# Moving a seventh of a depthwise convolution's taps from VectorE to ScalarE and adding DMAs, in a fused attention and ConvNeXt kernel

## The chip, the cores and the metric

The kernel runs on one core of one Trainium2 chip. The metric is the device time of one execution in microseconds (us), lower is better. The time before is 3349.05 us, the median of three runs (3346.46 to 3350.15). The engines are named as in the profile: PE is the matrix engine, PEld its weight loads, DVE is VectorE, ACT is ScalarE, POOL is GpSimd and SP is SyncE. POOL and SP do hardly anything here but issue DMAs.

## The reference, cut to what matters

Two layers run one after the other on a batch of 8 images of 384 channels and 32 x 32 pixels, all in float32.

```python
# layer 0: attention and MLP over the 1024 pixels ("tokens") of an image
xn = layernorm(xf, g1, beta1)                  # over the 384 channels
q, k, v = split(xn @ w_qkv.T + b_qkv)          # 8 heads of 48
out = softmax(q @ k.T * SCALE) @ v
x1 = out @ w_proj.T + b_proj + xf
h = gelu(layernorm(x1, g2, beta2) @ w_fc1.T + b_fc1)    # 384 -> 1536
x = x1 + h @ w_fc2.T + b_fc2                            # 1536 -> 384
# layer 1: ConvNeXt block
y = depthwise_conv_7x7(x, dw_w) + dw_b         # 49 taps, each channel by itself
y = layernorm(y, ln_w, ln_b)
y = gelu(y @ w1 + b1)                          # 384 -> 1536
gx = sqrt(sum over pixels of y ** 2); nx = gx / (mean of gx + eps)
y = grn_gamma * (y * nx) + grn_beta + y
out = x + y @ w2 + b2                          # 1536 -> 384
```

## The kernel before, in words

**Layout.** Channels lie on the 128 partitions, in CT = 3 channel tiles (`ct`), and the 1024 pixels of an image along the free axis, in two halves of NH = 512. A float32 matmul over 512 columns is two MATMUL rows in the profile. The images are worked off one after the other, and the two layers overlap: while PE does layer 0 of image b, the convolution of image b-1 runs beside it. For an image in the middle PE's order is: `values` and `qk` (the projections), `attention` (64 steps of scores and products, four pairs of heads for each half of the queries), `mlp` (fc1 of half 0, then of half 1, then fc2), `grn_up` and `grn_down` of the image before (layer 1's two matmuls). fc2, w1 and w2 are done by fast-matrix-product forms (`by_thirds`, `grn_up`), which need extra sums on DVE and adding DMAs on POOL.

**The plan.** The program is written in a fixed order for each engine; every engine then runs its own list in order and waits on semaphores. Work beside the matmuls is written as Python generators, and the class `Flow` decides where their instructions are put: `flow.pe(us)` moves a planned clock on by the planned time of a matmul (U = 0.857 us for 512 columns) and steps every chain that has come due. `yield 3.4` means that the chain's next instructions are put 3.4 planned us further on between the matmuls. A chain that was spawned as paced keeps its rhythm by that clock. `flow.finish(chain)` puts all that is left of a chain at once. The numbers behind `yield` are therefore guesses of a latency: when one is too short, the engine that gets the next instruction stands and waits with all that is queued behind it.

**The convolution.** `pad` holds the image with a border of 3. `convolution` makes 49 taps for each of the 3 channel tiles. A tap is one DVE instruction over all 1024 pixels, `acc = window * tap + acc`, 147 in all for an image, put `us` planned us apart and taken from the tiles in turn. It starts after `grn_up` (`start_conv`) and has to be done by the end of fc1 of the next image, where `next_norms` finishes it. The last image has none to overlap with: `last_convolution` works in two parts, rows 0 to 12 and rows 13 to 31, beside fc2 and the layer 1 of image 6 (`last`, which lies in the tile that held the qkv weights).

**The layernorms.** `layernorm` sums the three channel tiles on DVE, sums over the partitions with a matmul by a matrix of ones (`token_sums`), subtracts the mean (DVE), squares (ACT), sums again, takes Ln and Exp on ACT, and multiplies on DVE. With `fold` a DMA on POOL's queue first adds one half of the partitions to the other, and the matmuls have 64 rows and 64 columns, so that those of two pixel halves lie in different parts of the array. `abreast` runs both pixel halves side by side and stretches the waits by `factor`. Three layernorms occur for an image: ln1 (before `values`), ln2 (before fc1) and ln3 (after the convolution). ln3 stood unfolded and at the beginning of fc2.

**The averages.** `average` divides one pair of heads by its softmax sums: ACT and DVE add two PSUM banks, then come the sums by DMA to 128 partitions, a reciprocal on DVE, two more DMA steps through DRAM, and a multiplication on DVE. Its three waits were 2.8, 2.0 and 2.4. `ORDER[-1]` is the pair that comes last in a half; `proj` follows close behind it.

**Tags.** A tile pool hands out its buffers in turn by tag, and an instruction that writes a buffer waits until its last reader is done. `three.tile(..., tag="res")` had 3 buffers of 128 x 512.

Of the kernel before, what the change touches and what calls it, by code (L numbers as in the profile page):

```python
# [51 lines left out]
P = 128  # L52
# [14 lines left out]
U = 0.857  # L67
SCALE = HD ** -0.5
# [82 lines left out]
def block_kernel(  # L151
# [25 lines left out]
    flow = Flow()  # L177
    s_fc2 = dram.tile([P, len(FORMS), 4 * P], F32, tag="s_fc2", bufs=1, name="s_fc2")
# [188 lines left out]
    def token_sums(t, name, fold):  # L367

        width = t.shape[-1]
        if fold is None:
            total = o_tile(name)[:, :width]
            nc.tensor.matmul(out=total, lhsT=ones, rhs=t, start=True, stop=True)  # L374
            flow.pe(U * width / NH)
            return [(total, slice(0, width))]
        rows = [slice(0, 64), slice(64, P)]
        parts = [(fold, slice(0, width))]
        if fold == "columns":
            parts = [(j, slice(j * width // 2, (j + 1) * width // 2)) for j in range(2)]  # L380
        for j, cols in parts:
            nc.gpsimd.dma_start(out=t[rows[j], cols], in_=t[rows[1 - j], cols], accum_op=ALU.add)
        yield 3.4
        totals = []
        for j, cols in parts:
            total = o_tile(f"{name}_{j}")[:, : cols.stop - cols.start]
            for i in rows:
                nc.tensor.matmul(out=total[i, :], lhsT=ones[rows[j], :64], rhs=t[rows[j], cols], start=True, stop=True)
            flow.pe(U * width / NH / 2)
            totals.append((total, cols))  # L390
        return totals

    def layernorm(src, dst, h, eps, g, name, switch, spare=None, spaced=False, slow=1.0, fold=None, gentle=False):
# [17 lines left out]
        totals = yield from token_sums(a, f"{name}_sum{h}", fold)  # L411
# [20 lines left out]
        totals = yield from token_sums(squares[0], f"{name}_var{h}", fold)  # L432
# [23 lines left out]
    def abreast(*args, places=averages, fold=True, gentle=False, factor=1.4):  # L456

        chains = [
            layernorm(*args[:2], h, *args[2:], spare=places if h else None, fold=h if fold else None, gentle=gentle)
            for h in range(2)  # L460
        ]
        while chains:
            waits = []
            for chain in list(chains):
                wait = next(chain, None)
                if wait is None:
                    chains.remove(chain)
                else:
                    waits.append(wait)
            if waits:  # L470
                yield factor * max(waits)
# [75 lines left out]
    def average(b, qh, m, outs, sums, backs):  # L547


        tag = f"{b}_{qh}_{m}"  # L550
        nc.scalar.copy(attn[:, m, :], outs[0])  # L551
        yield 0.6
        nc.vector.tensor_tensor(attn[:, m, :], outs[1], attn[:, m, :], ALU.add)  # L553
        at = (qh * NP + m) * 8
        part = sums[:, at : at + 8]
        rows = attn[HD : HD + 65 : 64, m, :]
        nc.sync.dma_start(out=part, in_=rows.rearrange("j (a e) -> j a e", e=8))
        yield 2.8
        inv = small.tile([P, 8], F32, tag="inv", name=f"inv_{tag}")
        nc.vector.reciprocal(inv, part)  # L560
        back = backs[m] = dram.tile([2, NH], F32, tag=f"back{m}", name=f"back_{tag}")
        nc.sync.dma_start(out=back.rearrange("j (a e) -> (j a) e", e=8), in_=inv)
        if m == NP - 1:
            return
        while NP - 1 not in backs:
            yield 1.0
        for i, (own, other) in enumerate(pieces(lambda k: attn[:, k, :])):
            if i // 2 == m:
                nc.sync.dma_start(out=other, in_=own)
        yield 2.0  # L570
        r = two.tile([P, NH], F32, tag="r", name=f"r_{tag}")
        for j in range(2):
            nc.sync.dma_start(out=r[64 * j : 64 * j + HD, :], in_=back[j : j + 1, :].to_broadcast((HD, NH)))
            head = (2 * m + j) // CT
            nc.sync.dma_start(
                out=r[64 * j + HD : 64 * j + 64, :], in_=backs[NP - 1][head : head + 1, :].to_broadcast((16, NH))
            )
        yield 2.4
        nc.vector.tensor_tensor(attn[:, m, :], attn[:, m, :], r, ALU.mult)  # L579

    def attention(b, xt, qT, kT, last_tile, first):
# [44 lines left out]
        for n in range(len(steps) + 2):  # L626
# [4 lines left out]
            if n >= 2:  # L631
                product(*steps[n - 2], ps.pop(n - 2))
            if n - 2 == len(steps) // 2 + 6:
# [6 lines left out]
                slow = 1.4 if b in (1, B - 1) else 1.0  # L640
                ln = layernorm(xt, xn, 0, eps0, "g2", f"ln2_{b}", False, spaced=True, slow=slow, fold="columns")
                ln = flow.spawn(ln)

        def rest():
# [6 lines left out]
            proj(b, xt, 1)  # L651

# [65 lines left out]
    def mlp(b, xt, xn, weights, tag, ln, rest, before_fc2):  # L718
# [5 lines left out]
        for m in range(HT):  # L724
            gelu_half(hid, m, 0, xn, weights, wa, f"fc1_{b}")
            if m == 3 and rest:
                rest()
                slow = 1.2 if b == 1 else 1.0
                ln = flow.spawn(layernorm(xt, xn, 1, eps0, "g2", f"ln2_{b}", True, slow=slow))
        flow.finish(ln)  # L730
# [118 lines left out]
    def mlp_by_halves(b, xt, xn, weights, ln, rest, between):  # L849

        hid = one.tile([P, HT * N], F32, tag="big", name=f"hid_{b}").rearrange("p (m n) -> p m n", m=HT)
        for h in range(2):
            wa, wb = f"fc1_{b}_{h}", f"fc2_{b}_{h}"
            flow.finish(ln)
            for m in range(HT):
# [6 lines left out]
                if m == 6 and h == 0:  # L862
# [17 lines left out]
    def convolution(acc, us, slow=0, y0=0, y1=H, ready=tuple(range(CT))):  # L880
# [5 lines left out]
        while min(done) < KS * KS:  # L886
            left = [c for c in ready if done[c] < KS * KS]
# [12 lines left out]
            yield 2.43 if n <= CT * slow else us  # L900

# [78 lines left out]
    def grn_down_straight(b, y, kept, weights, tag, index, todo):  # L980
# [5 lines left out]
        def load():  # L986
            if len(res) < len(todo):
                r, part = todo[len(res)]
                t = three.tile([P, NH], F32, tag="res", name=f"res_{b}_{r}_{part.start}")[:, : part.stop - part.start]
# [165 lines left out]
    def prepare(weights, aside):  # L1155
# [25 lines left out]
        def spare(name):  # L1181
            return three.tile([P, NH], F32, tag="res", name=name)
# [122 lines left out]
    def main():  # L1305
# [41 lines left out]
        state = {"xn": xn, "conv": None, "acc": None, "norm1": None, "norm3": None}  # L1347
        kept = {}

        def start_conv(b, us, slow=0):  # L1350
            state["acc"] = one.tile([P, CT, N], F32, tag="acc", name=f"acc_{b}")
            state["conv"] = flow.spawn(convolution(state["acc"], us, slow), paced=True)

        def next_norms(b, ln=None):

            if b > 0:
                acc = state["acc"]
                flow.finish(state["conv"])
                norm = abreast(acc, acc, eps1, "lnw", f"ln3_{b - 1}", True, fold=False)
                norm = sequence(norm, block_differences(acc)) if b < B - 1 else after(ln, norm)  # L1360
                state["norm3"] = flow.spawn(norm)
# [22 lines left out]
        def last_convolution(h, ct, ln=None):  # L1384
            if ct < 0:
                next_norms(B - 1, ln)
                return
            ready[h].append(ct)
            if ct == 0:
                rows = (LAST[0].stop // W, H) if h else (0, LAST[0].stop // W)  # L1390
                conv = convolution(last, 0.86 if h else 0.6, 0, *rows, ready[h])
# [4 lines left out]
        for b in range(B):  # L1396
# [6 lines left out]
            if b < B - 1:  # L1403
                mlp(b, xt, xn, weights, b, ln2, rest, lambda: next_norms(b))
# [6 lines left out]
            if b == 0:  # L1411
                xt = load_x(b + 1, "x")
                flow.finish(preparing)
                start_conv(b, 1.6)
# [5 lines left out]
            if b < B - 1:  # L1420
                y, gx = grn_up(b - 1, acc, weights, b - 1)
                start_conv(b, 1.5 if b == B - 2 else 1.8, 10)
                scale = flow.spawn(grn_scale(b - 1, gx, weights, b - 1, y))
                next_values(b + 1)
                flow.finish(scale)
                grn_down(b - 1, y, xt, weights, b - 1, b - 1)
                xt = load_x(b + 1, "x")
# [35 lines left out]
    def exact_path():  # L1463

        load_wqkv(nc.scalar, nc.scalar)
        with tc.For_i(0, B) as b:
# [11 lines left out]
            mlp("x", xt, xn, weights, "x", ln, None, None)  # L1478
# [111 lines left out]
```

## Time and profile before

| what | from the profile before |
|---|---|
| profiled execution, its own time | 3348.34 us (span 3346.6 us) |
| PE busy | 3303.6 us, 99% of the span |
| DVE busy | 2550.6 us, 76% |
| ACT busy | 1421.0 us, 42% |
| POOL busy | 208.1 us, 6% |
| taps of images 0 to 6 (L897, 128 x 1024) | 1008 rows, 1230.6 us busy, 1276 ns each |
| taps of image 7 (L897, 128 x 416 and 128 x 608) | 288 rows, 193.7 us busy |
| from the start of qk to the next one, image 1 | 350.13 to 760.90: 410.8 us |
| the same, image 2 | 760.90 to 1165.17: 404.3 us |
| the same, image 3 | 1165.17 to 1569.43: 404.3 us |
| from the start of image 7's qk to the end | 2782.04 to 3346.6: 564.6 us |

The span is counted from the first to the last instruction. A busy PE row is modelled at its end, so the distance from one start to the next tells what a matmul costs: about 0.43 us for a row of 512 columns. Idle time of an engine that is not last anywhere costs nothing.

### The profile page before, as it was taken

The page shows a single profiled execution, that of the slowest core. Times are in us where ns is not written, and L with a number is a line of the kernel's source. Part 1 is how long each engine was busy: PE and PEld are TensorE (multiplying, and loading weights), DVE is VectorE, ACT ScalarE, POOL GpSimd, SP SyncE. Part 2 cuts the span into 40 slices and gives each one's busy share as a digit, 9 for nine tenths or more (in the row PEclk, how much of TensorE's full clock was granted, in tenths as well). Part 3 has the DMA queues.
Part 4 walks back from the last instruction along what each step waited for, and adds up shares of the span by engine and source line. Part 5 has one row for each costly group of instructions (what it writes and reads, how often), then busy time and mean ns, then how long its engine had stood idle before and what let it go on. Part 6 is the DMA issues. An engine that isn't in the chain of part 4 may idle for free.

```text
span 3346.6 us, 37477 instructions
## 1 busy us (share of the span) xinstructions
PE 3303.6 (99%) x14282; PEld 1416.7 (42%) x14282; DVE 2550.6 (76%) x3133; ACT 1421.0 (42%) x1884; POOL 208.1 (6%) x243
## 2 busy tenths in 40 slices
PE   8999999999999999999999999999999999999999
PEld 4344434443344433444334443444434444334455
DVE  4344788887877878779797796967888779989950
ACT  3442453444534354352552625426254353522641
POOL 2121000100000000100001000010000110000000
PEclk9999999999999999999999999999999999999999
DMA  5336102642125410445005350062501633023231
GB/s 185 111 105 148 52 20 57 158 102 63 25 70 146 115 47 20 105 122 135 20 16 131 96 140 17 17 157 80 128 18 37 170 83 95 20 56 90 62 98 50
DMA packets 151243, 281.59 MB, mean 84 GB/s; under 512 B 35216, under 2 KB 41232, under 8 KB 150672
## 3 DMA queue, kind: packets, MB, share of 16 engines
q1 hardware_dynamic: 114704, 201.32, 19.6%
q0 software_dynamic: 36064, 77.08, 11.9%
q8 instruction: 115, 1.88, 0.2%
q10 hardware_dynamic: 288, 0.71, 0.1%
q14 instruction: 72, 0.59, 0.1%
HBM read 181.52 MB, written 33.82 MB: 64 GB/s over the span
## 4 chain that ended last, share of the span: by engine, by line
PE 87%; DVE 10%; DMA 2%; issue 1%; ACT 0%; SPq 0%; POOL 0%; DVEq 0%; POOLq 0%
PE o L612 12%; PE s L592 12%; PE fc L345 12%; PE h L352 10%; PE fc_p L352 10%; PE o_p L352 9%; PE qk L332 6%; DVE wqkv L897 4%; PE v L521 4%; PE o L1000 4%; PE proj L535 3%; DVE acc L897 3%; PE h_last L1044 1%; PE qk_last L345 1%; PE ln_var L374 1%
## 5 line engine op out<-in xcount | busy, mean ns | idle before, releaser
L897 DVE SCALAR_TENSOR_TENSOR acc<-pad,vec,acc 128x1024 f32<-128x1024 f32 x1008 | 1230.6, 1276 | 0.0
L601 ACT ACTIVATE p<-s 128x1024 f32<-128x1024 f32 x512 | 523.6, 1024 | 380.6 <-PE s L592 378.4
L592 PE MATMUL s<-qk 48*64 48x512 f32 x4096 | 544.0, 592 | 1.6 <-ACT qk L495 1.5
L612 PE MATMUL o<-p,v 64*64 64x512 f32 x4096 | 538.9, 590 | 0.0
L345 PE MATMUL fc<-xn,fc 128*128 128x512 f32 x1152 | 500.4, 593 | 0.0
L345 PEld LDWEIGHTS fc<-xn,fc 128*128 128x128 f32 x1152 | 218.2, 190 | 278.2 <-issue 268.2
L352 PE MATMUL fc_p<-hid,fc 128*128 128x512 f32 x728 | 318.1, 592 | 0.0
L364 ACT ACTIVATE hid<-fc,bfc_f 128x512 f32<-128x512 f32 x192 | 130.9, 687 | 357.5 <-PE fc L345 357.4
L612 PEld LDWEIGHTS o<-p,v 64*64 64x64 f32 x4096 | 158.6, 133 | 284.6 <-issue 278.1
L592 PEld LDWEIGHTS s<-qk 48*64 48x64 f32 x4096 | 155.5, 133 | 286.0 <-issue 264.3
L945 DVE TENSOR_TENSOR y<-h,y 128x512 f32<-128x512 f32 x288 | 197.2, 690 | 97.8 <-PE h L352 87.3
L352 PE MATMUL o_p<-y,w 128*128 128x512 f32 x624 | 270.9, 592 | 0.0
L352 PEld LDWEIGHTS fc_p<-hid,fc 128*128 128x128 f32 x728 | 138.2, 190 | 174.4 <-issue 170.4
L332 PE MATMUL qk<-xn,wqkv 128*128 128x512 f32 x480 | 207.4, 592 | 0.0
L352 PE MATMUL h<-acc,w_A 128*128 128x512 f32 x432 | 206.4, 596 | 0.0
L897 DVE SCALAR_TENSOR_TENSOR wqkv<-pad,vec,wqkv 128x416 f32<-128x416 f32 (+1 forms) x288 | 193.7, 749 | 0.6
L352 PEld LDWEIGHTS o_p<-y,w 128*128 128x128 f32 x624 | 118.0, 190 | 148.7 <-issue 133.5
L553 DVE TENSOR_TENSOR attn<-o,attn 128x512 f32<-128x512 f32 x64 | 44.1, 689 | 147.2 <-ACT attn L551 147.2
L495 ACT ACTIVATE qk<-qk,bqk 128x1024 f32<-128x1024 f32 x40 | 44.6, 1114 | 229.0 <-PE qk L332 229.0
L712 ACT COPY pad<-x 128x512 f32<-128x512 f32 x48 | 30.2, 635 | 258.3 <-DVE x L777 192.4
L332 PEld LDWEIGHTS qk<-xn,wqkv 128*128 128x128 f32 x480 | 91.1, 190 | 114.1 <-issue 112.0
L535 PE MATMUL proj<-attn,wproj_sb 128*128 128x512 f32 x288 | 129.2, 602 | 2.1 <-DVE attn L579 2.1
(296 smaller groups left out, 3342.5 us busy)
## 6 DMA issues: line engine op xcount, KB each, us to landing
w_A<-in_w SPq DMA_DIRECT2D x72, 384.0 KB, 3.2
fc<-s_fc SPq DMA_DIRECT2D x91, 256.0 KB, 2.8
hid<-hid POOLq DMA_DIRECT2D x42, 512.0 KB, 6.7
fc<-in_wfc SPq DMA_DIRECT2D x54, 384.0 KB, 5.7
w<-s_w SPq DMA_DIRECT2D x78, 256.0 KB, 2.7
y<-y POOLq DMA_DIRECT2D x36, 512.0 KB, 7.0
kept<-x SPq DMA_DIRECT2D x8, 1536.0 KB, 8.3
xn<-in_x SPq DMA_DIRECT2D x14, 768.0 KB, 7.0
```

What stands on the lines that cost most here:

```text
L332: nc.tensor.matmul(out=ps[:, half(h)], lhsT=lhsT(k), rhs=rhs(k)[:, half(h)], start=(k == 0), stop=(k == nk - 1),)
L345: nc.tensor.matmul(out=ps, lhsT=lhsT(k), rhs=rhs(k)[:, half(h)], start=(k == 0), stop=(k == nk - 1))
L352: nc.tensor.matmul(out=bank, lhsT=lhsT, rhs=rhs, start=k == 0, stop=k == len(pairs) - 1)
L364: nc.scalar.activation(dst, src, function, **kw)
L521: nc.tensor.matmul(out=ps[:, :C], lhsT=xn[:, k, t * P : (t + 1) * P], rhs=wv_sb[:, k, :], start=(k == 0), stop=(k == CT - 1),)
L535: nc.tensor.matmul(out=ps, lhsT=wproj_sb[:, m, ct * P : (ct + 1) * P], rhs=attn[:, m, :], start=(m == 0), stop=(m == CT - 1),)
L592: nc.tensor.matmul(out=s[64 * i : 64 * i + 64, j, :], lhsT=kT[64 * j : 64 * j + HD, m, k0 : k0 + 64], rhs=qT[64 * j : 64 * j + HD, m, half ...
L601: nc.scalar.activation(p, s, AF.Exp)
L612: nc.tensor.matmul(out=outs[i][64 * j : 64 * j + 64, :], lhsT=v[keys, t, at : at + 64], rhs=p[keys, j, :], start=(t == 0), stop=(t == KT - 1),
L897: nc.vector.scalar_tensor_tensor(dst, window, tap, dst, ALU.mult, ALU.add)
L945: nc.vector.tensor_tensor(dst, bank, part, ALU.add)
L1000: nc.tensor.matmul(out=ps, lhsT=tiles[k], rhs=y(k, part), start=(k == 0), stop=(k == HT - 1))
```

## The change

1. **Taps.** For images 0 to 6 the last 7 of 49 taps (HELPED) of every channel tile are no longer made on DVE. `help_convolution` makes each of them in two halves of 512 pixels: ACT multiplies the window by the tap into a `res` tile (now 4 buffers), and a DMA on POOL's queue adds that tile to `acc`. It goes through the channel tiles 2, 1, 0, at 2.7 planned us a half tap. While a tile is being helped, and 8 us after, `taken` keeps DVE's taps off it. It pauses while `quiet` is not empty: through `grn_down`, and from the last nine steps of each half of the attention until `proj`.
2. **ln3.** It is started behind ln2's second half and the convolution, in fc1 of half 1 (`conv_norm`, called by `mlp` as `behind_ln`), no longer at the beginning of fc2, and it is folded. For image 7's pass it is started after the last step of fc1 of half 0 (m == HT - 1), where it was m == 6; it is folded too, with `factor=2.4`.
3. **Averages** of pairs that are not the last of a half wait 4.5, 3.0 and 5.0. ln2's first half waits 4.5 for its fold. The factor `slow` of its first half is 1.2 where it was 1.4 for images 1 and 7.
4. **Pacing.** The convolution's `us` is 1.65 for image 0 (was 1.6) and 1.8 for image 6 (was 1.5; others stay at 1.8); the last convolution's first part has 0.66 (was 0.6).

```diff
+HELPED = 7
-    def token_sums(t, name, fold):
+    def token_sums(t, name, fold, wait):
...
-        yield 3.4
+        yield wait
...
-        yield 2.8
+        yield 2.8 if hurry else 4.5
...
-        yield 2.0
+        yield 2.0 if hurry else 3.0
...
-        yield 2.4
+        yield 2.4 if hurry else 5.0
...
+            if n - 2 in (len(steps) // 2 - 9, len(steps) - 9):
+                quiet.append("averages")
...
                 proj(b, xt, 0)
-                slow = 1.4 if b in (1, B - 1) else 1.0
-                ln = layernorm(xt, xn, 0, eps0, "g2", f"ln2_{b}", False, spaced=True, slow=slow, fold="columns")
+                quiet.clear()
+                slow = 1.2 if b in (1, B - 1) else 1.0
+                ln = layernorm(xt, xn, 0, eps0, "g2", f"ln2_{b}", False, spaced=True, slow=slow, fold="columns", wait=4.5)
...
                 ln = flow.spawn(layernorm(xt, xn, 1, eps0, "g2", f"ln2_{b}", True, slow=slow))
+                behind_ln(ln)
...
-                if m == 6 and h == 0:
+                if m == HT - 1 and h == 0:
                     between(0, -1, ln)
...
+        taps = KS * KS - (HELPED if taken is not None else 0)
-        while min(done) < KS * KS:
-            left = [c for c in ready if done[c] < KS * KS]
+        while min(done) < taps:
+            left = [c for c in ready if done[c] < taps and not (taken and taken.get(c, 0) > flow.now)]
+            if not left:
+                yield 1.0
+                continue
...
+    def help_convolution(acc, us, taken):
+        yield 8.0
+        for ct in reversed(range(CT)):
+            taken[ct] = float("inf")
+            for i in range(KS * KS - HELPED, KS * KS):
+                dy, dx = divmod(i, KS)
+                for h in range(2):
+                    if quiet:
+                        while quiet:
+                            yield 1.0
+                        yield 3.0
+                    t = three.tile([P, NH], F32, tag="res", bufs=4, name=f"tap_{ct}_{i}_{h}")
+                    y0 = dy + h * H // 2
+                    window = pad[:, ct, y0 : y0 + H // 2, dx : dx + W]
+                    tap = col("dww", ct * KS * KS + i)
+                    nc.scalar.mul(t.rearrange("p (h w) -> p h w", w=W), window, tap)
+                    nc.gpsimd.dma_start(out=acc[:, ct, half(h)], in_=t, accum_op=ALU.add)
+                    yield us
+            taken[ct] = flow.now + 8.0
+        yield 8.0
+        taken.clear()
...
-        def next_norms(b, ln=None):
+        def conv_norm(b, ln):
             if b > 0:
                 acc = state["acc"]
+                how = dict(wait=5.0) if b < B - 1 else dict(wait=3.4, factor=2.4)
+                norm = abreast(acc, acc, eps1, "lnw", f"ln3_{b - 1}", True, **how)
+                if b < B - 1:
+                    norm = sequence(norm, block_differences(acc))
+                state["norm3"] = flow.spawn(after(ln, after(state["help"], after(state["conv"], norm))))
+        def next_norms(b):
+            if b > 0:
+                flow.finish(state["help"])
                 flow.finish(state["conv"])
-                norm = abreast(acc, acc, eps1, "lnw", f"ln3_{b - 1}", True, fold=False)
-                norm = sequence(norm, block_differences(acc)) if b < B - 1 else after(ln, norm)
-                state["norm3"] = flow.spawn(norm)
...
-                conv = convolution(last, 0.86 if h else 0.6, 0, *rows, ready[h])
+                conv = convolution(last, 0.86 if h else 0.66, 0, *rows, ready[h])
...
-                start_conv(b, 1.6)
+                start_conv(b, 1.65)
...
-                start_conv(b, 1.5 if b == B - 2 else 1.8, 10)
+                start_conv(b, 1.8, 10)
...
+                quiet.append("w2")
                 grn_down(b - 1, y, xt, weights, b - 1, b - 1)
+                quiet.clear()
```

## Prediction

> **What bounds the kernel now.** I read the busy shares, then PE's waits, then the stages, and last the few microseconds where PE waits longest.
>
> ```profile
> span 3346.6 us, 37477 instructions
> PE 3303.6 (99%) x14282; PEld 1416.7 (42%) x14282; DVE 2550.6 (76%) x3133; ACT 1421.0 (42%) x1884; POOL 208.1 (6%) x243
> ```
>
> PE is the bound. Who let it wait, in total, times and longest:
>
> ```profile
> PE ln_sum L374 <- DVE ln_a L409: 12.9, 5, 6.3
> PE ln_var L374 <- DVE ln_sq L430: 8.7, 8, 5.9
> ...
> PE ln_var L388 <- DMA ln_sq<-ln_sq: 2.2, 3, 1.2
> PE proj L535 <- DVE attn L579: 2.1, 1, 2.1
> PE h_last L1044 <- DVE wqkv L444: 1.6, 1, 1.6
> ```
>
> No wait names a tap of the convolution, but L409, L430 and L579 are DVE instructions that stand behind taps in DVE's list. By stage (PE, PEld, DVE, ACT, POOL busy; clock; DMA share; GB/s):
>
> ```profile
> 350.00:760.00 410.00, 405.89 (x1742) 169.20 (x1741) 337.76 (x385) 177.30 (x222) 23.29 (x22) 1.00 0.30 75
> 1266.00:1670.00 404.00, 403.63 (x1742) 169.00 (x1741) 324.36 (x377) 177.99 (x223) 23.35 (x22) 1.00 0.33 82
> 2883.00:3015.00 132.00, 123.02 (x581) 49.62 (x580) 114.36 (x146) 49.60 (x64) 3.34 (x4) 0.97 0.16 40
> 3015.00:3156.00 141.00, 139.17 (x330) 61.99 (x328) 140.13 (x222) 50.28 (x72) 0.00 (x0) 1.00 0.25 70
> ```
>
> In an image of the middle (second line) PE is busy for all but 0.4 of 404 us, DVE for 324. Less DVE work can give next to nothing there; only PE work that goes shortens it. Image 1 and the change to the last image have idle PE. In the last one (PE's own rows, idle time before in brackets):
>
> ```profile
> 2966.45 1.12 PE L374 MATMUL ln_sum<-ln_a,ones 128*128 128x512 f32 x2 [2.43 <-DVE ln_a L409]
> ...
> 3006.97 2.07 PE L374 MATMUL ln_var<-ln_sq,ones 128*128 128x512 f32 x2 [5.92 <-DVE ln_sq L430]
> 3008.83 1.76 PE L374 MATMUL ln_var<-attn,ones 128*128 128x512 f32 x2
> ...
> 3219.22 0.65 PE L374 MATMUL ln_sum<-ln_a,ones 128*128 128x288 f32 x2
> 3219.71 5.31 PE L1000 MATMUL o<-y,w_A 128*128 128x512 f32 x12
> 3224.86 0.65 PE L374 MATMUL ln_var<-ln_sq,ones 128*128 128x288 f32 x2
> ```
>
> **The change part by part.**
>
> *ln3 folded* (2 sums in each of 7 passes, 14 sets). Unfolded, the four rows of a set take 1.72 us (1392.06 to 1393.78 in PE's timeline). Folded sets stand in ln1: 1449.66 to 1450.74 is 1.08, and the rows before and behind come 0.09 and 0.11 late, so 1.28; another costs 1.22. A set saves 0.44 to 0.50, 14 save 6.2 to 7.0; I take **-6.5**. Bounds: 0, when the folding DMA is late at every set as at the worst fold (0.9 to 1.2 us), and -12.0, when a set took only one of two passes, 0.86. The trace shows less than that halving: a folded set is 1.22 to 1.28. The Trainium skill (TensorEngine Tiling (Array Packing), Key Properties and Theoretical Speedup) promises up to a doubling for a contraction of 64 rows, and says that changing the mode drains the engine. By its doubling the term would be -12.0; the two late rows are such a drain and eat part of it, so I keep the row.
>
> *Taps off DVE.* 7 x 3 for each of 7 images, 147 rows, follow each other at 1.196 us (three take 3.59 in the chain): 176 us less on DVE, 25 an image. In images 2 to 6 PE hides all of it but the 0.2 us wait of ln2's second half (L430), 0.2 to 0.4 an image: **-1.5** for five. Image 1 took 410.8 us from qk to qk, images 2 and 3 404.3. The 6.5 us are its waits for L579 (2.1), the fold (1.2), L430 (0.5) and the slow rows behind the first: after 2.08 us of idle PE five rows of proj start 0.85 us apart instead of 0.43. DVE gets 126 taps where it had 147, and the fold 4.5 where it had 3.4. Bounds 0 and -6.5; I take **-4**, since the averages' last pair, whose multiplication is L579, keeps its short waits.
>
> *The change to the last image.* ln2's second half waited 2.43 because three left-over taps were put at once into DVE's list ahead of its sums; in the new order finish() comes after fc1's last step, when those sums are through. ln3's second sum waited 5.92, behind taps put 0.6 apart while DVE had 20 other instructions in the same stretch; with 0.66 and factor 2.4 the sum comes some 10 planned us later. The 5.92 left PE slow: 3006.97 to 3010.43 is 3.46 for a set of 1.72. Together 2.5 + 5.9 + 1.7 = 10.1, and 0.6 for the fold at 2912 that gets a longer wait: **-10.7**. Bounds: 0, if 0.66 is still too dense (DVE is 140 of 141 us busy right behind), and -12.3 with L430's 1.4 at 3108.
>
> *What the slower pacing makes late.* The first part's 147 taps now take 0.06 longer each, 8.8 planned us, so the last convolution ends against PE's `finish` in front of `h_last` of part 1. In the program of before twelve rows of `o` (5.31 us, shown above) stood between the two sums of that layernorm. In the new program those twelve come before both sums, and nothing stands between. The whole chain is then bare: from the end of `o` to L1008, L406 and L409 1.9 (3214.0 to 3215.89), from the first sum to L430's end 3.0 (3219.22 to 3222.26), from the second sum to h_last 2.3 (3224.86 to 3227.13), 7.2 in all, of which PE works 1.0. It idles 6.2 where it idled 1.6: +4.6, and as behind 5.92 a slow set, up to 1.7: **+6.3**. Bounds +1 (taps early, half of the chain covered) and +9 (DVE 3 us late).
>
> *Half taps on ACT and POOL* (42 an image). The nearest ACT row is the copy into pad, 128 x 512, 635 ns: 27 us an image on an engine that is 178 of 404 busy. In the attention ACT runs an exp of 1.02 in every 1.72 and idles 0.70 before each, so a half tap fits into one gap, and at 2.7 apart there is one in about 1.6 steps. Where ln2's squares and an average's copy meet them, exps come late by some 0.5; PE needs an exp 2.6 after its scores, so 1.4 of lateness is free. The muls wait for a `res` buffer, that is for the DMA of four half taps earlier, 10.8 planned us. The DMA adds to the same 512 pixels every 5.4, in order. For 256 KB there is no row:
>
> ```profile
> hid<-hid POOLq DMA_DIRECT2D x42, 512.0 KB, 6.7
> y<-y POOLq DMA_DIRECT2D x36, 512.0 KB, 7.0
> ln_a<-ln_a POOLq DMA_DIRECT2D x16, 64.0 KB, 2.6
> ln_a<-ln_a POOLq DMA_DIRECT2D x7, 128.0 KB, 4.6
> ```
>
> The 64 KB rows are of the attention, where DMA share is 0.07 to 0.1; the long ones of stages with 0.5 to 1.1. I take 3 to 4 us, nearest to the row of the same stage. POOL's issue is 1.2 at most: 50 us of an idle queue. ln2's fold is behind it on POOL's list and gets 1.1 us more for it. SP's list gets nothing new; its small average DMAs share the 16 engines, with longer waits except for a half's last pair, when the helpers pause. Cost: **+2**, 0.3 an image; bounds 0 and +14 (2 us an image, as image 1's proj lost). The Trainium skill (ScalarE: Activation LUTs, Rules for kernel authors) speaks against this part: it sends multiplications to VectorE. By it the move would gain nothing, and per pixel the rows agree (635 for 512, 1276 for 1024 with an addition); what decides is which engine is waited for, and the table above names DVE.
>
> **Sum.** -6.5 - 1.5 - 4 - 10.7 + 6.3 + 2 = -14.4. The profiled execution took 3348.34 (0.7 below the median of 3349.05): **3334 us**.
>
> **Rivals.**
> - *Only PE's own work counts*: the last-image waits move instead of going, since the same 294 taps and ln3 stand in DVE's list. For: DVE is 140 of 141 busy. Against: the waits stand where taps and sums were put at once. -6.5 - 1.5 - 2 + 4.6 + 2 = -3.4: 3345, no change.
> - *Exps come late*: ACT's full list costs PE 2 us an image, +12 over the forecast: 3346. For: ACT's gap is 0.70 and a half tap 0.62; against: 1.4 of free lateness.
> - *The adding DMAs fall behind* (slower than before). From a landing of 5.4 us on, each DMA waits for the one before it; POOL's list shifts, `res` buffers come late, ACT stands with the exps behind it. At 6.4 it loses 0.5 for each half tap, 21 us an image, of which the buffers absorb 5 in each of the three tiles: 6 x 7 = 42, so 3376. For: the 512 KB rows land in 5.2 to 9.4. Against: those carry twice the bytes, in busier stages.
>
> **How the numbers follow.** Forecast 0.68, only PE's work 0.13, late exps 0.07, adding DMAs 0.12. 0.2% (6.7 us) is about what this measurement tells from no change, so faster means below 3342.3. The forecast's own bounds are 3348.3 - 7 - 2 - 6.5 - 11 + 3 = 3325 and, with the smaller gains, 3342. Both no-change rivals lie below 3350; above it are the slow rival and little else. Range 3324 to 3351, the forecast's own 3324 to 3342. Faster: the forecast and a little of the rest, 0.69; same 0.16; slower 0.15.
>
> **What would show it.** Right: an image of the middle near 402.9 from qk to qk; no wait of L374 on L409 or L430 around the beginning of the last convolution; a new wait of 5 to 7 us, in pieces, just before h_last of part 1; 256 KB adds landing in 3 to 4 us. Wrong: ACT waiting for DMAs among the exps; s or o rows with ACT named as their releaser; ln3's PE waits present in fc1. If images 2 to 6 grow instead of shrinking, the whole forecast is wrong.

## The result, and the profile after

The changed kernel takes 3333.85 us (median of four runs, 3333.69 to 3334.62) where the kernel before takes 3349.6 (four runs, one more than ahead of the prediction). The ratio is 0.9955, 95% interval 0.9938 to 0.9972. Measured again with later runs it was 3333.08 against 3347.89, ratio 0.9955 (0.9941 to 0.9968). The forecast was 3334, faster. The total is right; several of its terms are not, and they happen to cancel. The profiled execution took 3334.62 (span 3332.5), 14.1 us less in the span than before.

The busy shares, then PE's waits (engine, line waited for: total, times, longest), then the windows of image 1, of image 3 and of the last convolution (us, then PE, PEld, DVE, ACT, POOL busy, clock, DMA share, GB/s), then the new DMAs, all of the changed kernel:

```profile
span 3332.5 us, 38500 instructions
PE 3298.9 (99%) x14338; PEld 1418.3 (43%) x14338; DVE 2387.2 (72%) x2986; ACT 1593.0 (48%) x2180; POOL 480.9 (14%) x565
```

```profile
PE ln_sum L376 <- DVE ln_a L412: 12.0, 5, 6.2
PE ln_var L376 <- DVE ln_sq L433: 2.7, 2, 2.4
PE h_last L1081 <- DVE gmean L1098: 2.4, 1, 2.4
PE h_last L1081 <- DVE wqkv L447: 1.6, 1, 1.6
...
PE ln_sum L390 <- DMA ln_a<-ln_a: 1.2, 2, 0.8
```

```profile
346.60:750.50 403.90, 403.47 (x1751) 168.31 (x1750) 314.21 (x365) 202.30 (x265) 64.04 (x70) 1.00 0.49 107
1154.10:1558.30 404.20, 403.57 (x1752) 168.68 (x1751) 302.94 (x357) 202.27 (x264) 62.29 (x68) 1.00 0.49 111
...
3000.00:3120.00 120.00, 120.00 (x287) 52.98 (x286) 119.30 (x191) 46.49 (x63) 1.64 (x2) 1.00 0.25 71
```

```profile
acc<-tap POOLq DMA_DIRECT2D x294, 256.0 KB, 3.4
```

The waits of 5.9 (L430) and 2.1 (L579) are gone, and so is nearly all idle PE in image 1. The 256 KB adds land in 3.4 us, inside the estimate of 3 to 4. A wait for `gmean`, 0.4 before, is 2.4 now. By stretches, from the starts of PE's rows in the two traces (the column "forecast" puts the forecast's terms where they belong, the fold at 0.93 and the half taps at 0.3 an image):

| stretch | forecast | before | after | found |
|---|---|---|---|---|
| start to image 1's qk | 0 | 349.96 | 346.64 | -3.3 |
| image 1 | -4.6 | 410.77 | 403.89 | -6.9 |
| images 2 to 6 | -4.6 | 2021.1 | 2018.4 | -2.7 |
| image 7, qk to the first `h` | -11.3 | 299.8 | 287.7 | -12.1 |
| first `h` to `h_last` of part 0 | 0 | 65.2 | 63.2 | -2.0 |
| `h_last` to PE's last row | +6.3 | 192.1 | 201.9 | +9.9 |
| behind PE's last row | 0 | 7.6 | 10.7 | +3.1 |

In the last image the chain that ended last (start, us, engine, tile, line, instructions) runs on DVE from 2987 until `gmean`, and on PE from there. The 14 us that PE gained ahead of `h_last` met DVE's full list of taps:

```profile
3094.88 12.96 DVE wqkv L911 x17
3107.85 1.69 DVE wqkv L447 x3
3109.54 21.35 DVE wqkv L911 x28
3131.03 18.72 PE h_last L1081 x48
3149.75 51.52 PE o L1037 x120
```

Behind those rows of `o` stands the chain that the forecast calls bare, in PE's rows:

```profile
3202.95 0.75 PE L376 MATMUL ln_sum<-ln_a,ones 128*128 128x288 f32 x2 [1.70 <-DVE ln_a L412]
...
3206.15 1.31 PE L376 MATMUL ln_var<-ln_sq,ones 128*128 128x288 f32 x2 [2.45 <-DVE ln_sq L433]
...
3209.07 2.29 PE L1081 MATMUL h_last<-wqkv,w_A 128*128 128x288 f32 x4 [1.62 <-DVE wqkv L447]
```

The row of images 2 to 6 is the first clue that something is hidden: they shrank by 0.55 each (to 403.5 to 404.2, where the forecast's sign of being right was 402.9), though the fold alone should give 0.93 and ln2's wait 0.2 to 0.4. PE's waits show next to nothing there (0.4 us in image 3). This is ln3's first set of sums in image 4 of the changed kernel (timeline: start, us busy, engine, line, operation):

```profile
1768.67 1.08 PE L390 MATMUL ln_sum<-ln_a,ones 64*64 64x512 f32 x4
1769.70 1.08 PE L390 MATMUL ln_sum<-attn,ones 64*64 64x512 f32 x4
1769.80 2.48 DVE L419 SCALAR_TENSOR_TENSOR acc<-ln_sum,acc 128x512 f32<-128x512 f32 x4 [15.02 <-PE ln_sum L390]
1770.71 1.56 PE L347 MATMUL fc<-xn,fc 128*128 128x512 f32 x3
```

The rows of the two pixel halves (`ln_a` and `attn`) should run side by side in different parts of the array. Here four rows of one half run, and then four of the other: 2.04 us from the first to the next `fc`, where a folded set of ln1 takes 1.02. The fold of the second half was issued at 1763.37 and landed 6.2 us later, at 1769.57, too late for the second group to start beside the first. PE is not idle here, since the first half's rows are at work meanwhile; of the five such sets of ln3 only image 3's has a wait, of 0.44. Counted with the rows at its edges such a set costs 2.15 to 2.80 in images 2 to 6; a whole one costs 1.23, an unfolded one 1.73.

### The profile page after: what moved, and what is told of

It reads as the page before. It is cut to its first block, busy times and chain, and to the rows that moved or that the text cites. A ratio compares the mean times of both kernels' runs of the same rounds, so it can differ in the third digit from the quotient of the medians.

```text
span 3332.5 us, 38500 instructions
## 1 busy us (share of the span) xinstructions
PE 3298.9 (99%) x14338; PEld 1418.3 (43%) x14338; DVE 2387.2 (72%) x2986; ACT 1593.0 (48%) x2180; POOL 480.9 (14%) x565
## 4 chain that ended last, share of the span: by engine, by line
PE 82%; DVE 6%; issue 2%; ACT 0%; DMA 0%; SPq 0%; POOL 0%; DVEq 0%; POOLq 0%
PE s L597 11%; PE o L617 11%; PE fc L347 10%; PE h L354 10%; PE fc_p L354 10%; PE o_p L354 9%; PE qk L334 5%; DVE wqkv L911 4%; PE o L1037 4%; PE v L525 3%; PE proj L539 3%; PE h_last L1081 2%; PE qk_last L347 1%; DVE acc L911 1%; PE ln_sum L390 1%
## 5 line engine op out<-in xcount | busy, mean ns | idle before, releaser
L911 DVE SCALAR_TENSOR_TENSOR acc<-pad,vec,acc 128x1024 f32<-128x1024 f32 x861 | 1061.0, 1276 | 27.8 <-DMA acc<-tap 24.0
L933 POOL DMA_DIRECT2D acc<-tap x294 | 254.2, 870 | 1164.3 <-ACT tap L932 735.1
L932 ACT ACTIVATE tap<-pad,vec 128x512 f32<-128x512 f32 x294 | 210.3, 724 | 1.8 <-DMA acc<-tap 1.8
L911 DVE SCALAR_TENSOR_TENSOR wqkv<-pad,vec,wqkv 128x416 f32<-128x416 f32 (+1 forms) x288 | 193.5, 747 | 0.5
L558 DVE TENSOR_TENSOR attn<-o,attn 128x512 f32<-128x512 f32 x64 | 44.2, 690 | 181.9 <-ACT attn L556 181.1
```

The lines of the kernel that those rows point to most:

```text
L911: nc.vector.scalar_tensor_tensor(dst, window, tap, dst, ALU.mult, ALU.add)
L932: nc.scalar.mul(t.rearrange("p (h w) -> p h w", w=W), window, tap)
L933: nc.gpsimd.dma_start(out=acc[:, ct, half(h)], in_=t, accum_op=ALU.add)
```

## Experiments

All times are medians; "the kernel before" ran beside each and took 3346.8 to 3347.9. "Help" is ACT's multiplications with the adding DMAs.

### 1 The same kernel again, and a longer wait for ln3's fold

```diff
-                how = dict(wait=5.0) if b < B - 1 else dict(wait=3.4, factor=2.4)
+                how = dict(wait=7.0) if b < B - 1 else dict(wait=3.4, factor=2.4)
```

> The changed kernel with one number changed: ln3 of images 0 to 5 waits 7.0 planned us for its fold, not 5.0. In the changed kernel the set of ln3's first sums took 2.0 to 2.1 us in images 2 to 6, where folded sets elsewhere take 1.02: the second half's rows start 0.47 us behind the first half's, not 0.007, and its folding DMA lands (6.2 us after its issue, at 1769.57) just before they start (1769.70). Theory L (the late landing splits the set, with PE never idle): all sets take 1.02, images 2 to 6 lose 0.9 to 1.6 each, 5.3 in all: 3328.5. Rival O (the set is split because each half has a wait of its own in PE's list, whenever the DMA lands): no change, 3334. Rival K (ln3 ends later and grn_up then waits for it): images 2 to 6 grow by up to 2 each: 3334 to 3344.

(The first row of the second half starts 1.03 us behind the first row of the first half, not 0.47.) Measured 3329.15, ratio 0.9940 (0.9923 to 0.9956); images 2 to 6 take 402.57 each. To be sure of the difference, both kernels then ran on one chip:

> The changed kernel as it is, on the chip of the three runs beside it, so that they can be set against it and not only against the kernel before. 3334 +- 2 if chips differ as little as the two rows of medians of the kernel before (3349.6 and 3346.9). Its waits should be the same ones: 0.5 to 1 us more for a split set of ln3's first sums in each of images 2 to 6, 2.4 for gmean, 1.7 + 2.4 + 1.6 in front of h_last of part 1.

> The wait of 7.0 for ln3's fold once more, beside the changed kernel on one chip. Theory L (the late landing of the second half's fold splits the set): 4.5 to 5.3 us less than the changed kernel, images 2 to 6 at 402.6. If the first comparison only showed the difference of two chips, 0.

3333.08 (3331.08 to 3336.53) and 3328.74 (3325.86 to 3330.43): 4.3 us, without overlap. The same set with the longer wait:

```profile
1770.25 0.65 PE L390 MATMUL ln_sum<-ln_a,ones 64*64 64x512 f32 x2
1770.26 0.65 PE L390 MATMUL ln_sum<-attn,ones 64*64 64x512 f32 x2
1770.73 0.60 PE L390 MATMUL ln_sum<-ln_a,ones 64*64 64x512 f32 x2
1770.74 0.60 PE L390 MATMUL ln_sum<-attn,ones 64*64 64x512 f32 x2
```

The halves alternate, 0.01 apart. In the program the two matmuls of the first half stand ahead of the two of the second (`token_sums`) in both kernels, so it is not the planner that changed their order. Theory L holds: the late landing splits the set. Rival O (two waits in PE's list split it in any case) and rival K fall. An image of the middle is then accounted for: 404.27 - 1.0 (two sets at 1.23 for 1.73) - 0.45 (ln2's second sum with its wait) - 0.2 in `h`, which I did not trace = 402.6.

### 2 Help and averages, one at a time

Without the help (all 49 taps on DVE):

```diff
-            state["conv"] = flow.spawn(convolution(acc, us, slow, taken=taken), paced=True)
-            state["help"] = flow.spawn(help_convolution(acc, 2.7, taken), paced=True)
+            state["conv"] = flow.spawn(convolution(acc, us, slow), paced=True)
+            state["help"] = None
...
```

The lines that are not shown no longer wait for the help.

> The changed kernel with all 49 taps on DVE again; ln3, the averages and the pacing stay as changed. Theory F (the forecast's terms): the taps gave 1.5 us in images 2 to 6, 4 in image 1 and cost 2, so this takes 3334 + 3.5 = 3337, with image 1 at about 408 us from qk to qk (403.9 with the help) and images 2 to 6 at 403.9. Theory S (from the two traces): the end of the program is also 3.1 us longer since POOL has 294 more DMAs to see through its last drain (6.27 us against 3.78, and 1.70 against 1.09 for the instruction before it), so without them the stretch behind PE's last row is back at 7.4 us from 10.5, and the time is 3334 to 3335 even if image 1 loses its 4. Theory N (the waits of the averages alone cleared image 1): image 1 stays at 404 and the time is 3331.

With the help and the averages' old waits for all pairs:

```diff
-        hurry = m == ORDER[-1]
+        hurry = True
```

> The changed kernel with the averages' three waits back at 2.8, 2.0 and 2.4 for all pairs. In the traces DVE stood 76.3 us for the averages' last DMA (L579 behind r<-back) before the change and 26.7 after it (L584). Theory W (the longer waits are worth something by themselves: what stands behind such an instruction in DVE's list, b_f in image 0 and ln2's sums in image 1, came late for PE): DVE's wait for r<-back goes up to 70 or so, image 0 loses the 3.3 us that the forecast had no term for (313.8 from qk to qk against 309.9), image 1 loses 2 to 4, the others nothing: 3339 to 3341. Rival T (the taps that left DVE did it): image 1 stays at 404, image 0 at 310, as there are no taps in image 0 at all and 42 half taps are out of DVE's list in image 1: 3334. Rival Z (image 0's 3.3 us is an accident of one execution of the kernel before): image 0 stays at 310, image 1 loses 2 to 4: 3336 to 3338.

With neither (both edits):

> The changed kernel without the help (all 49 taps on DVE) and with the averages' short waits: only ln3's fold and place, ln2's factors and the pacing are left of the change. With the changed kernel (help and long waits, 3333), the one without the help (long waits, 3341) and the one with short waits (with help, 3356) it closes a square. Theory I (the adding DMAs are what makes the short waits too short): without them the long waits are worth little, as in the kernel before, where PE waited for an average in one place only (2.1 us, image 1) and for b_f (3.3): 3341 + 3 to 6 = 3344 to 3347. Theory W (the short waits cost the same with and without help): 3341 + 23 = 3364.

With help and old waits, the adds left out:

```diff
-                    nc.gpsimd.dma_start(out=acc[:, ct, half(h)], in_=t, accum_op=ALU.add)
```

> The kernel with help and short waits (3356), with ACT's 294 multiplications in place and their adding DMAs left out: 7 of 49 taps then do not reach the output, and POOL and the DMA engines have 77 MB less to move. In images 2 to 6 PE waited 1.1 to 3.2 us for the last average (proj behind L584), 11 us in all, and each was 1.4 to 4.2 longer than with long waits. Theory I (the 256 KB adds hold up the averages' small DMAs, whose longest landings went from 1.4 to 3.1, from 2.0 to 3.4 and from 2.1 to 3.5 us in image 3): these waits go, images 2 to 6 are back at 403 to 404, image 1 at 406 or less, 3356 - 12 to 18 = 3338 to 3344. Theory A (ACT's multiplications stand ahead of the averages' copies in ACT's list): nothing goes, 3356 +- 2.

| | old short waits | long waits |
|---|---|---|
| taps all on DVE | 3351.6 (ratio 1.0011, 1.0002 to 1.0021) | 3341.0 (0.9980, 0.9970 to 0.9989) |
| help, adds left out | 3343.5 (0.9988, 0.9979 to 0.9998) | not run |
| help | 3356.1 (1.0022, 1.0012 to 1.0031) | 3333.1 (0.9955, 0.9941 to 0.9968) |

The cells ran on three chips, so differences of 1 us among them say little. The longer waits are worth 10.6 us without the help and 23.0 with it; no theory had both, and none of the three for help with short waits came near 3356. Taps that leave DVE are worth 8.1 when the adds are left out, and the adds then cost 12.6. Of the 12.1 us between the two profiled executions, 3.1 lie in image 0, ahead of the first add (ACT's first helped tap starts at 346.3 us), so the adds' own cost is nearer to 9. With long waits the help is worth 7.9, about what the taps alone gave. This speaks for long waits making the adds nearly free, but it is not shown, as help with long waits and without adds was not run.

The 7.9 is also net of a loss. Without the help images 2 to 6 take 403.2 to 403.5 each, less than with it, and their first sets are whole: those sums stand 231 us after the qk, some 20 behind the issue of the fold, where with the help they stand at 210, 5 behind it.

With help and short waits, PE and DVE wait as follows:

```profile
PE proj L539 <- DVE attn L584: 13.4, 6, 3.2
...
DVE attn L584 <- DMA r<-back: 107.5, 46, 6.6
```

With the adds left out, the same two are

```profile
PE proj L539 <- DVE attn L584: 6.8, 4, 2.3
...
DVE attn L584 <- DMA r<-back: 89.3, 42, 6.5
```

This is how it comes about with the adds, in DVE's timeline of image 2:

```profile
916.05 0.69 DVE L584 TENSOR_TENSOR attn<-attn,r 128x512 f32<-128x512 f32 x1 [2.85 <-DMA r<-back]
916.65 2.48 DVE L911 SCALAR_TENSOR_TENSOR acc<-pad,vec,acc 128x1024 f32<-128x1024 f32 x2
919.05 0.68 DVE L558 TENSOR_TENSOR attn<-o,attn 128x512 f32<-128x512 f32 x1
...
927.91 0.69 DVE L584 TENSOR_TENSOR attn<-attn,r 128x512 f32<-128x512 f32 x1 [0.90 <-DMA r<-back]
```

DVE stands 2.85 for one pair's DMA; the first addition of the last pair (L558) is queued behind it, and the last pair's multiplication comes at 165.7 us after image 2's qk instead of 160.5 as in the changed kernel, and `proj` waits 3.2 us for it. In image 3 the longest landings of the averages' three kinds of small DMA are 1.4, 2.0 and 2.1 us without adds and 3.1, 3.4 and 3.5 with them. Over images 2 to 6, 5 of the 98 whose landing the trace shows take more than 2.5 us without adds and 28 with them; the longest is 3.5 and 3.9, and the medians differ by 0.2 at most. DVE also waits for the adds themselves, 23.7 us in all with short waits; the changed kernel has this too (24.0) with no wait for `proj`, so it is not enough by itself. DVE's total wait for `r` was 76.3 us before the change and is 26.7 after it. Theory I is right for some 9 to 12 us, but not for all: with the adds left out PE still waited 6.8 us for `proj` in four images, and 3.3 in four with neither help nor long waits, where the kernel before waited 2.1 in one. What causes that remainder is open.

Theory S for the run without help was wrong in size (3334 to 3335 expected, 3341 measured). Image 1 took 408.1, and the stretch behind PE's last row was back at 7.7, both as expected. What it missed stands in the last image: layer 1 of image 6 begins at 297.9 us after the qk and not at 287.7, with this in PE's waits:

```profile
PE fc L347 <- DVE acc L419: 6.1, 1, 6.1
...
PE fc L347 <- DVE x L725: 1.7, 1, 1.7
```

### 3 The help alone

The kernel before with `help_convolution`, its pauses and the fourth buffer, nothing else.

> The kernel before with the help alone (taps on ACT and adding DMAs, the pauses, the fourth buffer); ln3, the waits and the pacing are those of before. The forecast's terms for this part alone: 1.5 + 4 - 2 = 3.5 us less, 3344. Theory I (adds and short waits together make the averages late for proj): images 2 to 6 grow by 2 to 4 each as in the kernel with short waits, 3348 + 8 to 15 = 3356 to 3363. For the last image: if the help of image 6's convolution is what took its waits of 2.4 and 5.9 away, layer 1 of image 6 starts at 290 us after the qk of image 7 or before, as it does with the whole change (287.7); if the pace and the later start did it, at 298 or after, as before (299.8).

Measured 3360.3, ratio 1.0035 (1.0022 to 1.0048): slower than the kernel before by 13.6 us, where the forecast's terms said 3344. Theory I had the size, but the place is another: PE hardly waits for `proj`; it waits 0.8 to 1.3 us in each of images 2 to 6 for ln2's fold, which stands on POOL's queue with the adds (405.1 from qk to qk, +0.9):

```profile
1300.68 0.77 PE L390 MATMUL ln_var<-ln_sq,ones 64*64 64x256 f32 x6 [0.79 <-DMA ln_sq<-ln_sq]
```

The change gives this fold 4.5 instead of 3.4. Images 2 to 6 make 5.3 of the 12.0 us between the two profiled executions; the rest stands in image 0 (2.7), image 1 (1.5), the last image up to the first `h` (2.7) and behind PE's last row (2.0), less 2 elsewhere. In the last image the first `h` is at 302.5, and the 5.9 of L430 are there. With the pace and the later start alone (the run without help) it was at 297.9, with waits of 6.1 and 1.7; only with both is it 287.7.

### 4 The end of the last convolution

The first part's pace put back:

```diff
-                conv = convolution(last, 0.86 if h else 0.66, 0, *rows, ready[h])
+                conv = convolution(last, 0.86 if h else 0.6, 0, *rows, ready[h])
```

> The changed kernel with one number put back: the taps of the last convolution's first part stand 0.6 planned us apart, not 0.66. In PE's order this puts rows of o between the two sums in front of h_last of part 1 again. Theory P (the forecast: the slower pace is what made this chain bare, for 4.6 to 6.3 us): the chain is covered again, 3334 - 5 = 3329, unless ln3's second sum gets its wait of 5.9 back, which stands beside it and shows separately. Theory D (DVE has no idle time between 232 and 388 us after the qk of image 7, so its last tap starts at 431 whatever the pace): last tap at 431 +- 1, PE waits for the same time in other places, 3334 +- 1.

Measured 3337.8, ratio 0.9965 (0.9951 to 0.9979): some 4 us slower than the changed kernel, though on another chip, and neither theory's number. The chain is covered again in part, as P said (the first of its three waits is gone and the second is 1.8, not 2.45; from the first `o` to `h_last` of part 1 it is 56.3 us, not 59.5; the last tap is at 427.7, so D's 431 is wrong), but the denser taps cost more elsewhere:

```profile
3058.29 9.65 DVE L911 SCALAR_TENSOR_TENSOR wqkv<-pad,vec,wqkv 128x416 f32<-128x416 f32 x17
...
3067.84 0.75 DVE L725 SCALAR_TENSOR_TENSOR x<-fc,vec,x 128x512 f32<-128x512 f32 x1
...
3068.63 0.63 ACT L721 COPY pad<-x 128x512 f32<-128x512 f32 x1 [9.59 <-DVE x L725]
...
3071.50 3.78 PE L334 MATMUL h<-acc,w_A 128*128 128x512 f32 x4 [4.86 <-ACT h L1013]
```

17 taps stand ahead of fc2's last addition in DVE's list; ACT stands 9.59 us for that addition, with the gelus of `h` behind it, and PE stands 4.86 for a gelu.

Then the second part's pace instead, together with the wait of 7.0:

```diff
-                conv = convolution(last, 0.86 if h else 0.66, 0, *rows, ready[h])
+                conv = convolution(last, 0.78 if h else 0.66, 0, *rows, ready[h])
```

> The wait of 7.0 for ln3's fold, and the taps of the last convolution's second part stand 0.78 planned us apart, not 0.86; the first part stays at 0.66. In PE's order the sums in front of h_last of part 1 then come 8 and 0 matmuls of o before its end: the first link of the chain is covered. Theory P (the chain is bare because it is put late): of the waits of 1.7, 2.4 and 1.6 the first two go, 4 us, and gmean's wait grows by 1 to 3 since some 4 more taps stand ahead of it: 3329 - 1 to 3 = 3326 to 3328. Theory D (DVE's list is full up to its last tap at 429 us after the qk of image 7): the last tap stays at 429 +- 1, the sums wait for it where they now stand, inside o, and the time stays at 3329 +- 1 or gets worse by gmean's wait. Where DVE stood 3.55 us for PE's first block of o, at 391 us, tells them apart: by P that idle time fills with taps and the last one comes at 425 to 426.

Measured 3326.12 (ratio 0.9936, 0.9921 to 0.9952), 2.6 below the kernel with 7.0 alone on the same chip (3328.74). The last tap is at 424.9 and the second sum's wait is gone, as P said; the first sum still waits 1.06 where P had no wait, and the gmean wait fell to 1.3 where P had it grow, but PE then stands 1.6 for an ACT instruction behind it. PE's rows of that stretch:

```profile
3189.66 0.75 PE L376 MATMUL ln_sum<-ln_a,ones 128*128 128x288 f32 x2 [1.06 <-DVE ln_a L412]
3190.25 7.03 PE L1037 MATMUL o<-y,w_A 128*128 128x512 f32 x16
...
3197.12 0.65 PE L376 MATMUL ln_var<-ln_sq,ones 128*128 128x288 f32 x2
...
3199.39 2.94 PE L1081 MATMUL h_last<-wqkv,w_A 128*128 128x288 f32 x11 [1.62 <-DVE wqkv L447]
```

Help for the last convolution too (5 taps of its first part, one 416-pixel add each, written like `help_convolution`):

```diff
+            if ct == CT - 1 and h == 0:
+                state["help"] = flow.spawn(help_last(last, 2.7, last_taken, 5, 0, LAST[0].stop // W), paced=True)
...
```

> The changed kernel, and in addition 5 of the 49 taps of the last convolution's first part (13 rows, 416 pixels) go to ACT and adding DMAs for each channel tile: 15 DVE instructions of 0.566 us, 8.5 us, are gone. Theory D (DVE's full list sets the end of the last convolution: its last tap starts 431.15 us after the qk of image 7 before the change and 431.11 after it, though PE reached layer 1 of image 6 12 us earlier): the last tap comes 8 us earlier, the waits for gmean (2.4) and in front of h_last of part 1 (5.8) shrink, time 3334 - 6 to 8 = 3326 to 3328. Rival P (the taps are where the planner's pace of 0.66 puts them, and DVE merely follows): the last tap is also earlier, by 15 x 0.66 = 9.9, so this run alone can't tell P from D; the run with the pace at 0.6 does. Rival A (ACT or the adding DMAs stand in the way of the gelus and of the norm of part 0): no gain or a loss, 3334 to 3338.

Measured 3343.6 (0.9983, 0.9974 to 0.9993), 10 us slower than the changed kernel: rival A, and by more than it said.

```profile
3030.91 0.66 ACT L950 ACTIVATE last_tap<-pad,vec 128x416 f32<-128x416 f32 x1 [4.40 <-DMA wqkv<-last_tap]
...
3035.66 1.74 POOL L951 DMA_DIRECT2D wqkv<-last_tap  x2 [2.83 <-DVE wqkv L911]
...
3041.26 4.78 DVE L911 SCALAR_TENSOR_TENSOR wqkv<-pad,vec,wqkv 128x416 f32<-128x416 f32 x7 [2.82 <-DMA wqkv<-last_tap]
...
3074.97 5.61 PE L334 MATMUL h<-acc,w_A 128*128 128x512 f32 x8 [8.19 <-ACT h L1031]
```

DVE, which is behind its plan here, holds up the adds (POOL waits for L911), the adds hold up ACT by the buffers and DVE by the order on the tile, and the gelus stand behind ACT's taps. DVE lost 11.5 us in three such waits and gained 8.5.

### 5 A second fold with the same fault

On top of the wait of 7.0 and the pace of 0.78:

```diff
-                norm = abreast(xn, xn, eps0, "g1", name, True, places=places, gentle=b > 0, factor=1.4 if b else 1.7)
+                norm = abreast(xn, xn, eps0, "g1", name, True, places=places, gentle=b > 0, wait=3.4 if b else 4.4, factor=1.4 if b else 1.7)
```

> The kernel with 7.0 for ln3's fold and 0.78 for the last convolution's second part (3326), and the same cure in a third place: ln1 of image 1, in image 0's fc2, waits 4.4 planned us for its fold, not 3.4 (times its factor 1.7). There PE waits 0.8 us for the fold of the first sums and 0.3 to 1.0 between the halves of the second set, with three to six slow rows behind it. Theory L (a fold that lands late costs its wait, the split set and the slow rows): 2 to 4 us less, 3322 to 3324, image 0 at 306 to 308 from qk to qk. Rival: the layernorm ends later and values of image 1, 15 us on, waits for it: 3326 +- 2.

Measured 3320.43 (3317.36 to 3320.93), ratio 0.9914 (0.9901 to 0.9928). This version is 0.9% faster than the kernel before and 13 us below the changed one. Image 1's ln1 in image 0 had both faults, the wait and the split; first the changed kernel, then this one:

```profile
297.00 1.08 PE L390 MATMUL ln_sum<-ln_a,ones 64*64 64x512 f32 x4 [0.83 <-DMA ln_a<-ln_a]
298.03 1.08 PE L390 MATMUL ln_sum<-attn,ones 64*64 64x512 f32 x4
```

```profile
297.36 0.65 PE L390 MATMUL ln_sum<-ln_a,ones 64*64 64x512 f32 x2
297.37 0.65 PE L390 MATMUL ln_sum<-attn,ones 64*64 64x512 f32 x2
```

The first set costs 1.23 where it cost 3.14, the second 1.23 where it cost 2.85; image 0 takes 306.4 from qk to qk, 3.0 less than with 7.0 and 0.78 alone, as expected. The median fell by 5.7, more than that, but the two ran on different chips. PE got no wait for image 1's `values`, so the rival falls.

## Why the prediction was right, and where it was not

- **The fold of ln3 (-6.5).** The mechanism and the price of a whole set are right: 0.50 saved, 1.23 for 1.73. The step that failed is the lower bound: "0, when the folding DMA is late at every set" left out that a late fold on one half costs more than the unfolded set, in four of five cases without any idle PE. In the changed kernel five of the 14 sets cost 0.4 to 1.1 more than before, 3.0 in all, and nine saved 0.5: -1.5, not -6.5. The longer wait brings 4.3 to 4.7 of the missing 5.0.
- **Packing.** The Trainium skill (TensorEngine Tiling (Array Packing), Theoretical Speedup) has up to a doubling, by which the term was -12.0. Whole sets give a factor of 1.4 (1.73 to 1.23), so the measurement decides.
- **Taps off DVE (-4 in image 1).** Right in size: without the help image 1 takes 408.1, with it 403.9. But it takes both parts: with the help and short waits it is 408.7. The term left out image 6's taps, which decide over the last image (10 us of it). The Trainium skill's rule (ScalarE: Activation LUTs, Rules for kernel authors) to leave multiplications to VectorE, by which the prediction said that nothing would be gained, does not hold here: 7.9 us with the long waits.
- **Averages.** The forecast used their longer waits only as cover for the adds' "+2". They have a worth of their own (10.6 us without the help), and image 0 has it too: DVE stood 6.7 us for `r` with `b_f` behind it and PE stood 3.3 for that. The five programs with short waits take 313.1 to 318.2 for image 0, eight profiles with long ones 309.2 to 312.1. That image's -3.3 had no term, and its size is loose: the changed kernel took 309.9 and 312.0 in its two profiles. The cost of +2 for the half taps was not measured by itself with the long waits; with the old ones the adds cost up to 12.6.
- **The change to the last image (-10.7).** Right in size (-12.1 with the fold, and the 1.4 of L430 that the bounds named came on top at `h`). The cause was half told: it named the pace and the later `finish`; the two runs with one half each show that neither these nor the taps do it alone.
- **The bare chain (+6.3).** Right: idle 1.70 + 2.45 + 1.62 = 5.8 for the 6.2 forecast, and with the slow rows 6.1 more than before. That it comes from where the chain is put is shown by the run with 0.78, where only the waits of 1.06 and 1.62 are left. What was missed is one step earlier: `gmean`, 3.7 with its slow rows. The chain that ended last, shown above, is DVE's up to that point. That is the part of the rival "only PE's own work counts" that came true.
- **Behind PE's last row (+3.1).** Not in the forecast.
- **Rivals.** Late exps: not seen. A helped half tap took 0.72 on ACT, more than the 0.62 of the rival and the gap of 0.70, but PE's waits for ACT are the 1.5 us for `qk` that stood there before, and ACT waited 1.8 us in all for an adding DMA. Adds that fall behind: the median landing is 3.4, below the 5.4 from which that rival begins, though 21 of 294 took longer, up to 9.4.
- **The landing.** The prediction says that there is no row of 256 KB. The list of before has such rows, of copies without an addition, with medians from 2.3 (`s_fc`) to 13.3 (`fc_a`); the estimate of 3 to 4 held without them.

Terms missed for the good (image 0 -3.3, image 1 and `h` -4) and for the bad (fold 5, gmean 3.7, the end 3.1) are of the same size; that 3334 came out is partly luck.

## What to carry to other kernels

Where two halves are to run side by side in the array, look at the order of their rows, not at idle PE: x4 and x4 instead of x2 alternating is a late operand. A planned wait that is too short puts an instruction at the head of an in-order list, and its price is paid by what is queued behind it; when DMAs are added to a stretch, the waits for the DMAs that were there need to grow with them: here the added DMAs with the old waits were slower than neither (3356 and 3352). Before work is moved to a second engine, see whether the engine that it must keep step with is behind its plan there.

## What the runs showed of the hardware that I had not expected

- A split set costs 0.9 to 1.0 us more than a whole one with PE busy throughout (1.6 where a wait of 0.44 came on top); a list of idle times does not show the former.
- The end of the program depends on something other than PE's work: POOL's last long drain took 3.8 us with 222 DMAs on its queue in the kernel before, 6.3 with 544 in the changed kernel (6.27 in every profile of a kernel with 544), 5.1 with 516, but 1.5 with 250 and 1.2 with 559. The last of these still needed 9.5 us behind PE's last row, and three programs with 250 needed 7.7, 7.7 and 9.7. It goes with the program and not simply with the number of DMAs; what sets it is open.
- Adds of 256 KB hardly move the medians of small DMAs beside them (by 0.2 us at most), but they make long landings common (28 of 98 above 2.5 us instead of 5), and a list in order pays the long ones.
